# Giving the difference tiles a pool of their own, and ordering the last stage of a fused transformer kernel by hand

## The chip, the core and the metric

The kernel runs on one core of a Trainium2 chip. Its engines are TensorE (PE; weight loads are shown as PEld), VectorE (DVE), ScalarE (ACT), GpSimd (POOL) and SyncE (SP), which here only starts DMAs. The metric is the device time of one execution in microseconds, median of several runs. Times inside an execution come from a hardware profile of one of them.

## The reference

The input is `x`, 64 batches of 32 heads of 512 values, 2048 tokens in all, in float32. Two layers are applied, each with a residual:

```python
x = x + _L0_ffn_ref(_L0_cond_ref(x, lengths, ...), ...)   # long convolution, then a linear layer with routed LoRA
x = x + _L1_ffn_ref(_L1_cond_ref(x, ..., indices, 0), ...)  # gated layer with LoRA by batch, then the mixture below
```

The part that matters here is the last one, a mixture of 16 experts with two chosen for each token, beside a shared expert that all tokens use:

```python
gu_s = x2 @ shared_w_gate_up.T
g_s, u_s = jnp.split(gu_s, 2, axis=-1)
shared_out = silu(g_s) * u_s @ shared_w_down.T
...                                   # softmax, top 2, weights normalised to 1
gu = einsum('th,eih->eti', x2, w_gate_up)
act = silu(g) * u
out_e = einsum('eti,ehi->eth', act, w_down)
moe_out = einsum('eth,te->th', out_e, combine)
return moe_out + shared_out
```

## The kernel before

Tokens lie along the free dimension for most of the work: `xall` holds 4 blocks of 512 features (`NC` = 4 chunks of 128 partitions), and a token block `tb` (0 to 3) is 8 heads of all 64 batches, 512 tokens.

The first layer comes first. Then the gated layer of the second runs over 8 groups `g` of 8 batches, with 11 slices `j` of its hidden width in each. Its gate and up products use Strassen's scheme with seven products in place of eight, which needs sums of weight quarters and differences of input quarters. `differ(g)` (L789) makes the differences of a group on VectorE, in a tile `t` of the pool `l1c`; `combine_shared(j)` (L801) makes four sums of the weights of the shared expert's slice `j`, for j = 1, 2 and 3, in the last group, one call behind each of the slices 1, 2 and 3. The sums of slice 3 are made in another `t` tile and stored in DRAM (`shared_d`), because their room is wanted for other things in between. The adapters' product `lo` (L835) is made once for four slices.

After the last group `begun()` (L1140) starts the shared expert on token block 0: it finishes the last group (`past.down`, `own`, `adapt`, `turn`), closes `l1c`, opens the pool `early` with two buffers of 8 KB per partition, and makes the differences for block 0 (`differing`, L1035) in the first of them, `t_0`. `adapt` stores the group's finished rows `zt` to DRAM (`zd`) through SP's queue, just ahead of 16 loads of expert weights (`wall`). A new pool that lies over a closed one waits for the last users of all the closed pool's tiles, by the addresses of the two pools.

`shared(tb)` (L1077) runs the shared expert for one block. For slice 0 it makes gate and up by plain products (`gate_up`, L779); for slices 1 to 3 by `seven` (L1047), whose four calls of `products` write four PSUM banks; VectorE adds them up (L1064 to L1066 after the second, L1069 and L1070 after the third, L1072 and L1073 after the fourth), ScalarE applies silu (L1117) and VectorE multiplies (L1118). The down projection (L1093) of a slice follows the products of the next slice. `done(step, j)` calls a hook at a named point. PSUM has eight banks: two in the pool `ps_mm`, two in `ps_td`, four in `ps_acc`; the down projection holds those four.

The order of the work: in a `manual_schedule` region, PE, VectorE and ScalarE issue their instructions in the order in which they are written. The region runs from the start up to the end of `shared(1)`. What follows is ordered by the compiler's own planner: `worked` (L1343), which takes the 42 tiles of 128 rows through the experts, and the last stage. `issue_after` queues instructions behind a given one of the same engine.

The last stage: `shared(2)` and `shared(3)`; the gathers of each token's two expert rows from `yd` by indirect DMA on GpSimd (`rows_of`, L1414; 16 pairs of tiles, 32 gathers); the weighing of a pair (`weighed`: a scaling, L1421, and a scaled add, L1422); and `routed`, which turns the weighed rows by 64 transposes (L1441), 16 for each token block, adds them to the block's result (L1442) and stores it (L1444). A one-element memset (L1412) in front of a gather makes the gather wait for VectorE's place in the order. In this version three pairs are gathered at a time and up to four weighed at a time, behind the multiply L1118 of a slice; all 64 transposes are written behind slice 1 of `shared(3)`. The planner puts the down projection of slice 0 ahead of them and mixes that of slice 1 among them.

Of the kernel before, what the change touches and what calls it, by code (L numbers as in the profile page):

```python
# [9 lines left out]
F32 = mybir.dt.float32  # L10
I32 = mybir.dt.int32
AF = mybir.ActivationFunctionType
ALU = mybir.AluOpType
# [4 lines left out]
P = 128  # L18
B, H, L = 64, 32, 512
NS = 64  # L20
TB, NTB = 512, 4
HB = TB // B
NC = L // P
NT = B * H // P
# [5 lines left out]
NS1 = 4  # L30
# [6 lines left out]
GB = 8  # L37
NG, TG = B // GB, GB * H
# [5 lines left out]
BW = L // 2  # L44
# [59 lines left out]
def kernel(ctx: ExitStack, tc: tile.TileContext, a: dict, out: bass.AP):  # L104
    nc = tc.nc
    mm, tt, ts = nc.tensor.matmul, nc.vector.tensor_tensor, nc.vector.tensor_scalar
# [10 lines left out]
    def bank(pool, name):  # L117
        return pool.tile([P, TB], F32, tag="bank", name=name)
# [13 lines left out]
    s4 = wl0.tile([P, 5, H], F32, name="s4")  # L132
# [656 lines left out]
    def differ(g):  # L789

        b11, b12, b21, b22 = (xall[:, k : k + 2, :, lo : lo + HG] for k in (0, 2) for lo in (g * GB, g * GB + HG))
        halves.append((b11, b12, b21, b22))
        t = l1.tile([P, 4, 2, P], F32, tag="t", name=f"t_{g}")
        t1, t2, t3, t4 = (t[:, i].rearrange("p c (h b) -> p c h b", b=HG) for i in range(4))
        differences.append([t[:, i] for i in range(4)])
        tt(t1, b12, b11, ALU.subtract)
        tt(t2, b22, t1, ALU.subtract)
        tt(t3, b22, b12, ALU.subtract)
        tt(t4, b21, t2, ALU.subtract)

    def combine_shared(j):  # L801


        if j == NS1 - 1:
            ssw.append(l1.tile([P, 4 * BW], F32, tag="t", name="ssw_made"))
        a11, a12, a21, a22 = (sw[j][:, i * BW : (i + 1) * BW] for i in range(4))
        s2, s3, s4 = (ssw[j - 1][:, i * BW : (i + 1) * BW] for i in range(3))
        tt(s3, a11, a21, ALU.subtract)
        tt(a21, a21, a22, ALU.add)
        tt(s2, a21, a11, ALU.subtract)  # L810
        tt(s4, a12, s2, ALU.subtract)
        if j == NS1 - 1:
            nc.sync.dma_start(shared_d, ssw[j - 1][:, 0 : 3 * BW])

# [26 lines left out]
    kept = ctx.enter_context(tc.tile_pool(name="kept", bufs=1))  # L841
    ssw = [kept.tile([P, 3 * BW], F32, name=f"ssw_{j}") for j in range(1, NS1 - 1)]
    l1s = ExitStack()
    l1 = l1s.enter_context(tc.tile_pool(name="l1c", bufs=2))

    def batches(g, c, half=None):
# [97 lines left out]
    for g in range(NG):  # L944
# [3 lines left out]
        for j in range(NF):  # L948
# [36 lines left out]
                combine(j + 2)  # L985
            if g + 1 < NG and j == 9:
                differ(g + 1)
            if g + 1 == NG and 1 <= j < NS1:
                combine_shared(j)
            if past is not None:  # L990
                if j == 0:
                    past.adapt()
# [54 lines left out]
    def seven(tb, j, banks, si, at, done):  # L1047

        b11, b12, b21, b22 = quarters(tb)
        t1, t2, t3, t4 = diffs[tb]  # L1050
        gate, up = (x.rearrange("p (k t) -> p k t", k=2) for x in (si, at))

        def products(k, *parts):
            ps = bank(banks[k % len(banks)], f"sgu_{tb}_{j}_{k}").rearrange("p (k t) -> p k t", k=2)
            for i, (w, x) in enumerate(parts):
                w = sw[j][:, w * BW :] if w < 4 else ssw[j - 1][:, (w - 4) * BW :]
                for c in range(2):
                    mm(ps[:, i, :], w[:, c * P : (c + 1) * P], x[:, c, :], start=(c == 0), stop=(c == 1))  # L1058
            return ps

        ps = products(0, (0, b11), (6, b22))
        nc.scalar.copy(gate, ps)
        ps = products(1, (1, b21), (4, t2))
        tt(up[:, 0], gate[:, 0], ps[:, 1], ALU.add)  # L1064
        tt(gate[:, 0], gate[:, 0], ps[:, 0], ALU.add)
        tt(gate[:, 1], gate[:, 1], up[:, 0], ALU.add)  # L1066
        done("gate", j)
        ps = products(2, (3, t4), (5, t3))
        tt(up[:, 1], up[:, 0], ps[:, 1], ALU.add)  # L1069
        tt(up[:, 0], up[:, 1], ps[:, 0], ALU.add)  # L1070
        ps = products(3, (2, t1))
        tt(gate[:, 1], gate[:, 1], ps[:, 0], ALU.add)  # L1072
        tt(up[:, 1], up[:, 1], ps[:, 0], ALU.add)  # L1073
# [3 lines left out]
    def shared(tb, behind=None, midway=None, hooks=None, first=None):  # L1077
# [19 lines left out]
        for j in range(NS1):  # L1097
            if j > 0:
                si = glu.tile([P, TB], F32, tag="si", name=f"ssi_{tb}_{j}")
                at = glu.tile([P, TB], F32, tag="at", name=f"sat_{tb}_{j}")  # L1100
                seven(tb, j, (ps_mm,) if hooks else (ps_mm, ps_mm, ps_td, ps_td), si, at, done)
                pair = [si, at]
            elif first is not None:
                pair = first()
            else:
                banks = ps_mm if hooks else (ps_mm, ps_td)[j % 2]
                pair = []
                for which in range(2):
                    pair.append(bank(banks, f"sgu_{tb}_{j}_{which}"))
                    gate_up(pair[-1], tb, j, which)  # L1110
                    if which == 0:
                        done("gate", j)
            done("products", j)
            if j == 0:
                si = glu.tile([P, TB], F32, tag="si", name=f"ssi_{tb}_{j}")
                at = glu.tile([P, TB], F32, tag="at", name=f"sat_{tb}_{j}")
            nc.scalar.activation(si, pair[0], AF.Silu)  # L1117
            product = tt(at, si, pair[1], ALU.mult)  # L1118
            if j == 0 and tb == 1:
                diffs[tb] = in_place_of(0)  # L1120
                run(differing(tb, diffs[tb]))
            if j == 0:
                x1 = pools[tb // 2].tile([P, NC, TB], F32, tag="acc", name=f"x1_{tb}")
                nc.sync.dma_start(x1, x1d[tb])
                acc.append(x1)
            done("up", j)
            if behind is not None:
                with tc.issue_after(product.ins):
                    behind(j)
            if before is not None:  # L1130
                down(j - 1, before)
            before = at
            if j == 1 and midway is not None:
                midway()
# [5 lines left out]
    def begun():  # L1140
# [15 lines left out]
        gate_up(pair[1], 0, 0, 1, range(3, NC), there)  # L1156
        past.turn()
        l1s.close()
        pools.append(ctx.enter_context(tc.tile_pool(name="early", bufs=2)))
        sums = routing.enter_context(tc.tile_pool(name="ssw", bufs=1))  # L1160
        ssw[-1] = sums.tile([P, 3 * BW], F32, name="ssw_last")
        nc.gpsimd.dma_start(ssw[-1], shared_d)
# [232 lines left out]
    worked(0, NTU, ahead[0], spare=last_differences())  # L1395
    experts.close()
    wide.close()
    pools.append(ctx.enter_context(tc.tile_pool(name="late_acc", bufs=2, side="right")))
    late = ctx.enter_context(tc.tile_pool(name="late", bufs=1, side="right"))
    ssw[-1] = late.tile([P, 3 * BW], F32, name="ssw_late")  # L1400
    nc.sync.dma_start(ssw[-1], shared_d)
    with tc.tile_pool(name="fin", bufs=NT) as fin:
        order = [q * NTB + tb for tb in range(NTB) for q in range(NTB)]
        pairs = []

        def rows_of(lo, hi, held=True):

            for n in order[lo:hi]:
                g = [fin.tile([P, L], F32, tag=f"g{k}", name=f"g{k}_{n}", bufs=(NT, 6)[k]) for k in range(2)]
                for k in range(2):  # L1410
                    if held:
                        nc.vector.memset(g[k][:, 0:1], 0.0)  # L1412
                    at = bass.IndirectOffsetOnAxis(ap=posi[:, k, n : n + 1], axis=0)
                    nc.gpsimd.indirect_dma_start(g[k], None, yd[:, :], at)  # L1414
                pairs.append(g)

        def weighed(lo, hi):

            for i in range(lo, hi):
                n, g = order[i], pairs[i]  # L1420
                ts(g[0], g[0], shr[:, 0, n : n + 1], None, ALU.mult)  # L1421
                stt(g[0], g[1], shr[:, 1, n : n + 1], g[0], ALU.mult, ALU.add)  # L1422

        cuts = (0, 0, 3, 6, 9, 13, NT)

        def sums(j):
            weighed(cuts[j], cuts[j + 1])
            rows_of(3 * (j + 1), min(3 * (j + 2), NT))

        rows_of(0, 3, held=False)  # L1430
        shared(2, behind=sums)

        def routed():

            for tb in range(NTB):
                for o in range(NC):
                    ps = bank((ps_mm, ps_td)[o % 2], f"moe_{tb}_{o}")
                    by_head = ps.rearrange("p (h b) -> p h b", b=B)
                    for q in range(4):
                        src = pairs[tb * 4 + q][0][:, o * P : (o + 1) * P]  # L1440
                        nc.tensor.transpose(by_head[:, :, q * 2 * GB : (q + 1) * 2 * GB], src, ident)  # L1441
                    tt(acc[tb][:, o, :], acc[tb][:, o, :], ps, ALU.add)  # L1442
                    if tb < NTB - 1:
                        nc.sync.dma_start(out[tb, :, o, :], acc[tb][:, o, :])  # L1444

        shared(3, behind=lambda j: sums(4 + j) if j < 2 else None, midway=routed)
        for o in range(NC):
            nc.sync.dma_start(out[3, :, o, :], acc[3][:, o, :])

# [94 lines left out]
```

## Time and profile before

| what | us |
|---|---|
| median of 3 runs (1025.9 to 1026.53) | 1025.91 |
| the profiled execution | 1026.44 |
| its span, first to last instruction | 1024.7 |
| PE busy | 989.9 |
| DVE busy | 649.0 |
| ACT busy | 212.1 |
| POOL busy | 170.0 |
| mean granted PE clock, as a share | 0.998 |

The span is cut into stages at about these times: first layer to 165, groups 0 to 7 to 708, `shared(0)` and `shared(1)` to 802, the experts to 937, `shared(2)` to 974, `shared(3)` with the transposes to 1020, the last adds and stores to the end. A line of a timeline gives start, duration, engine, line of the kernel, operation, what is written and read, and in brackets the idle time before it with what seems to have released it. Successive matmuls overlap, so distances between starts say more than durations. When a wait has several causes, the one named is the one that came last in the profile.

### The profile page before, as it was taken

The page shows a single profiled execution, that of the slowest core. Times are in us where ns is not written, and L with a number is a line of the kernel's source. Part 1 is how long each engine was busy: PE and PEld are TensorE (multiplying, and loading weights), DVE is VectorE, ACT ScalarE, POOL GpSimd, SP SyncE. Part 2 cuts the span into 40 slices and gives each one's busy share as a digit, 9 for nine tenths or more (in the row PEclk, how much of TensorE's full clock was granted, in tenths as well). Part 3 has the DMA queues.
Part 4 walks back from the last instruction along what each step waited for, and adds up shares of the span by engine and source line. Part 5 has one row for each costly group of instructions (what it writes and reads, how often), then busy time and mean ns, then how long its engine had stood idle before and what let it go on. Part 6 is the DMA issues. An engine that isn't in the chain of part 4 may idle for free. (4 is left out here: it accounts for less than half of the span.)

```text
span 1024.7 us, 16925 instructions
## 1 busy us (share of the span) xinstructions
PE 989.9 (97%) x6256; PEld 794.2 (78%) x6256; DVE 649.0 (63%) x1974; ACT 212.1 (21%) x439; POOL 170.0 (17%) x189
## 2 busy tenths in 40 slices
PE   3999999999999999999999999999899999999998
PEld 1777656888898889988899898897667677776665
DVE  6656567886666776666766767764775453333775
ACT  2322111121221311224112131211100222221100
POOL 2131001210301202102012031000000322221730
PEclk9999999999999999999999999999999999999999
DMA  6566308685756746746467566531930355555752
GB/s 186 189 223 232 135 20 310 234 295 173 227 182 193 259 158 215 247 157 232 154 219 256 160 212 216 166 124 52 418 141 1 117 167 167 172 166 202 201 170 96
DMA packets 64210, 190.62 MB, mean 186 GB/s; under 512 B 8512, under 2 KB 11616, under 8 KB 63488
## 3 DMA queue, kind: packets, MB, share of 16 engines
q1 hardware_dynamic: 49360, 138.30, 39.0%
q0 software_dynamic: 14176, 51.16, 16.2%
q8 instruction: 52, 0.85, 0.3%
q14 instruction: 30, 0.25, 0.1%
q10 hardware_dynamic: 592, 0.07, 0.1%
HBM read 158.35 MB, written 31.15 MB: 185 GB/s over the span
## 5 line engine op out<-in xcount | busy, mean ns | idle before, releaser
L883 PE MATMUL zp<-wn,at 128*128 128x288 f32 x704 | 185.4, 407 | 0.4 <-DVE at L982 0.4
L818 PE MATMUL gu<-t,w 128*128 128x128 f32 x1056 | 150.2, 278 | 0.9 <-DVE gus L964 0.9
L883 PEld LDWEIGHTS zp<-wn,at 128*128 128x128 f32 x704 | 127.2, 191 | 28.5 <-DVE at L982 0.6
L818 PEld LDWEIGHTS gu<-t,w 128*128 128x128 f32 x1056 | 135.4, 192 | 14.8 <-DVE gus L964 6.4
L444 POOL DMA_INDIRECT wa<-in_la,row_a x64 | 61.1, 955 | 299.9 <-issue 183.4
L980 ACT ACTIVATE si<-gus 128x256 f32<-128x256 f32 x88 | 36.7, 417 | 352.2 <-DVE gus L978 352.2
L818 PE MATMUL gum<-xall,w 128*128 128x128 f32 x704 | 93.0, 275 | 0.0
L818 PEld LDWEIGHTS gum<-xall,w 128*128 128x128 f32 x704 | 85.7, 192 | 0.0
L1320 PE MATMUL egu<-wall,zx 128*128 x336 | 80.6, 383 | 0.3 <-issue 0.3
L964 DVE TENSOR_TENSOR gus<-gu,los 128x512 f32<-128x512 f32 x88 | 60.5, 688 | 29.8 <-PE gu L818 27.3
L958 DVE TENSOR_TENSOR los<-los 128x512 f32<-128x512 f32 (+1 forms) x72 | 46.6, 647 | 48.6 <-ACT los L838 47.0
L1320 PEld LDWEIGHTS egu<-wall,zx 128*128 128x128 f32 x336 | 60.5, 190 | 19.9 <-ACT zx L1311 13.0
L982 DVE TENSOR_TENSOR at<-si,gus 128x256 f32<-128x256 f32 x88 | 37.4, 425 | 48.2 <-ACT si L980 48.2
L1301 POOL DMA_INDIRECT zr<-zd,tok x42 | 39.7, 945 | 164.0 <-PE zrp L1309 86.3
L838 ACT COPY los<-lo 128x512 f32<-128x512 f32 (+1 forms) x96 | 46.6, 561 | 59.5 <-PE lo L835 59.5
L1093 PE MATMUL op<-sat,sw 128*128 128x512 f32 x128 | 58.0, 595 | 0.6 <-DVE sat L1118 0.3
L589 PE MATMUL main<-yT,w 128*128 128x512 f32 x128 | 58.4, 599 | 0.0
L835 PEld LDWEIGHTS lo<-rs,wb 64*128 64x128 f32 x704 | 42.9, 188 | 16.9 <-issue 11.1
L835 PE MATMUL lo<-rs,wb 64*128 64x128 f32 x704 | 48.5, 280 | 6.9 <-DVE gus L978 6.2
L818 PE MATMUL gu<-xall,w 128*128 128x128 f32 x352 | 53.7, 275 | 0.0
L818 PE MATMUL gum<-t,w 128*128 128x128 f32 x352 | 53.7, 275 | 0.0
L1340 DVE COPY eys<-ey 128x512 f32<-128x512 f32 x42 | 29.0, 691 | 29.7 <-PE ey L1338 29.7
(316 smaller groups left out, 1456.2 us busy)
## 6 DMA issues: line engine op xcount, KB each, us to landing
w<-sums_d SPq DMA_DIRECT2D x77, 512.0 KB, 4.7
w<-in_cw SPq DMA_DIRECT2D x77, 384.0 KB, 3.6
wall<-in_xw SPq DMA_DIRECT2D x16, 768.0 KB, 15.1
yd<-eys SPq DMA_DIRECT2D x42, 256.0 KB, 2.8
g<-kpad SPq DMA_DIRECT2D x15, 512.0 KB, 5.6
w<-in_cw SPq DMA_DIRECT2D x11, 512.0 KB, 4.8
sums_d<-w SPq DMA_DIRECT2D x9, 512.0 KB, 3.9
xall<-in_xT SPq DMA_DIRECT2D x4, 1024.0 KB, 8.6
```

The source lines that it names most:

```text
L444: nc.gpsimd.indirect_dma_start(to, None, src, at)
L589: mm(ps, w0[:, c, o * P : (o + 1) * P], yT[:, c, :], start=(c == 0), stop=(c == NC - 1),)
L818: mm(to, block(n, i)[:, c * P : (c + 1) * P], x[:, c], start=(c == 0), stop=(c == 1))
L835: mm(banks[which][:, at : at + P], wb[mine, lo : lo + P], r[mine, half, :], start=True, stop=True)
L838: nc.scalar.copy(to[:, first - j : first - j + n, 2 * which : 2 * which + 2], src)
L883: mm(self.zp[half][s][:, 0 : DW - TW], at[:, 1 - half, :], wn[:, j, s, lo : lo + DW - TW], start=(j == 0), stop=(j == NF - 1),)
L958: tt(lo[:, :, i], lo[:, :, i], lo[:, :, less], ALU.subtract)
L964: tt(flat, ps, adapters[:, j % 4].rearrange("p k t -> p (k t)"), ALU.add)
L982: tt(at, si, flat[:, TG:], ALU.mult)
L1093: mm(op[o], sw[j][:, i : i + P], at, start=(j == 0), stop=(j == NS1 - 1))
L1301: nc.gpsimd.indirect_dma_start(zr, None, zd[:, :], bass.IndirectOffsetOnAxis(ap=tok[:, t : t + 1], axis=0))
L1320: mm(ps[:, 0:256], x[:, c, :], wflat()[:, bass.ds(start + c * 256, 256)], start=(c == 0), stop=(c == NC - 1))
```

## The change

Four edits:

1. The `t` tiles (differences, and the sums of slice 3) move from `l1c` to a pool `dif` of their own, opened ahead of it. The pool `early` with two buffers becomes two pools `early_0` and `early_1` with one each. `t_0` and later `x1_1` lie in `early_0`, `x1_0` in `early_1`.
2. `combine_shared` becomes a generator that yields after each of its four sums; the three calls are chained in the order 3, 1, 2, and from slice 1 of the last group on each slice takes two sums (one if j is 4 or 8).
3. The last stage, from behind `worked` on, is a `manual_schedule` region for PE, VectorE and ScalarE.
4. Two pairs are gathered first. Then a `step` is taken at each of the points ("up", 0), ("gate", j), ("mid", j) and ("up", j) of `shared(2)` and `shared(3)`, where "mid" is a new hook in `seven` behind L1070. A step gathers one pair and weighs the pair gathered three steps earlier. At ("up", j), behind the step and in front of the down projection of the slice before, `routed` turns one token block, if its four pairs are weighed.

```diff
-        t = l1.tile([P, 4, 2, P], F32, tag="t", name=f"t_{g}")
+        t = dif.tile([P, 4, 2, P], F32, tag="t", name=f"t_{g}")
...
+            assert len(ssw) == j - 1
+            ssw.append(dif.tile([P, 4 * BW], F32, tag="t", name="ssw_made"))
...
-        tt(s3, a11, a21, ALU.subtract)
...
+        yield tt(s3, a11, a21, ALU.subtract)
+        yield tt(a21, a21, a22, ALU.add)
+        yield tt(s2, a21, a11, ALU.subtract)
+        yield tt(s4, a12, s2, ALU.subtract)
...
+    dif = l1s.enter_context(tc.tile_pool(name="dif", bufs=2))
     l1 = l1s.enter_context(tc.tile_pool(name="l1c", bufs=2))
...
-            if g + 1 == NG and 1 <= j < NS1:
-                combine_shared(j)
+            if g + 1 == NG and j > 0:
+                sums = sums if j > 1 else (x for k in (3, 1, 2) for x in combine_shared(k))
+                next(sums, None)
+                if j % 4:
+                    next(sums, None)
...
         tt(up[:, 1], up[:, 0], ps[:, 1], ALU.add)
         tt(up[:, 0], up[:, 1], ps[:, 0], ALU.add)
+        done("mid", j)
...
-                x1 = pools[tb // 2].tile([P, NC, TB], F32, tag="acc", name=f"x1_{tb}")
+                x1 = pools[(1, 0, 2, 2)[tb]].tile([P, NC, TB], F32, tag="acc", name=f"x1_{tb}")
...
-        pools.append(ctx.enter_context(tc.tile_pool(name="early", bufs=2)))
+        for i in range(2):
+            pools.append(ctx.enter_context(tc.tile_pool(name=f"early_{i}", bufs=1)))
...
     worked(0, NTU, ahead[0], spare=last_differences())
     experts.close()
     wide.close()
+    ctx.enter_context(tc.manual_schedule(engines=by_hand))
...
+        def step():
+            if len(pairs) < NT:
+                rows_of(order[len(pairs)])
+            if len(weighed) < NT and (len(pairs) == NT and step.last or len(weighed) < len(pairs) - 3):
+                n, g = order[len(weighed)], pairs[len(weighed)]
+                ts(g[0], g[0], shr[:, 0, n : n + 1], None, ALU.mult)
+                stt(g[0], g[1], shr[:, 1, n : n + 1], g[0], ALU.mult, ALU.add)
+                weighed.append(g[0])
+            step.last = len(pairs) == NT
...
         def routed():
+            tb = len(turned_in)
+            if tb == NTB or len(weighed) < 4 * (tb + 1):
+                return
+            turned_in.append(tb)
...
+        hooks = {("up", 0): step}
+        for j in range(1, NS1):
+            hooks |= {(x, j): step for x in ("gate", "mid")} | {("up", j): step_and_block}
+        for _ in range(2):
+            rows_of(order[len(pairs)], held=False)
+        for tb in range(2, NTB):
+            shared(tb, hooks=hooks)
```

More of the change, by code (lines that the diff above doesn't have):

```diff
@@ L804, in combine_shared @@
         if j == NS1 - 1:
-            ssw.append(l1.tile([P, 4 * BW], F32, tag="t", name="ssw_made"))
+            assert len(ssw) == j - 1
+            ssw.append(dif.tile([P, 4 * BW], F32, tag="t", name="ssw_made"))
         a11, a12, a21, a22 = (sw[j][:, i * BW : (i + 1) * BW] for i in range(4))
         s2, s3, s4 = (ssw[j - 1][:, i * BW : (i + 1) * BW] for i in range(3))
-        tt(s3, a11, a21, ALU.subtract)
-        tt(a21, a21, a22, ALU.add)
-        tt(s2, a21, a11, ALU.subtract)
-        tt(s4, a12, s2, ALU.subtract)
+        yield tt(s3, a11, a21, ALU.subtract)
+        yield tt(a21, a21, a22, ALU.add)
+        yield tt(s2, a21, a11, ALU.subtract)
+        yield tt(s4, a12, s2, ALU.subtract)
         if j == NS1 - 1:
@@ L1100, in shared @@
                 at = glu.tile([P, TB], F32, tag="at", name=f"sat_{tb}_{j}")
-                seven(tb, j, (ps_mm,) if hooks else (ps_mm, ps_mm, ps_td, ps_td), si, at, done)
+                seven(tb, j, (ps_mm,) if tb < 2 else (ps_mm, ps_mm, ps_td, ps_td), si, at, done)
                 pair = [si, at]
@@ L1105, in shared @@
             else:
-                banks = ps_mm if hooks else (ps_mm, ps_td)[j % 2]
+                banks = ps_mm if tb < 2 else (ps_mm, ps_td)[j % 2]
                 pair = []
@@ L1403 @@
         order = [q * NTB + tb for tb in range(NTB) for q in range(NTB)]
[L1404 to L1415, printed above, removed]
@@ L1417, in weighed, with rows_of @@
-        def weighed(lo, hi):
-            for i in range(lo, hi):
-                n, g = order[i], pairs[i]
+        pairs, weighed, turned_in = [], [], []
+        def rows_of(n, held=True):
+            g = [fin.tile([P, L], F32, tag=f"g{k}", name=f"g{k}_{n}", bufs=(NT, 6)[k]) for k in range(2)]
+            for k in range(2):
+                if held:
+                    nc.vector.memset(g[k][:, 0:1], 0.0)
+                at = bass.IndirectOffsetOnAxis(ap=posi[:, k, n : n + 1], axis=0)
+                nc.gpsimd.indirect_dma_start(g[k], None, yd[:, :], at)
+            pairs.append(g)
@@ L1421, in weighed @@
+        def step():
[3 more added lines that the diff above has]
+                n, g = order[len(weighed)], pairs[len(weighed)]
                 ts(g[0], g[0], shr[:, 0, n : n + 1], None, ALU.mult)
                 stt(g[0], g[1], shr[:, 1, n : n + 1], g[0], ALU.mult, ALU.add)
[L1424 to L1428, printed above, removed]
@@ L1430 @@
-        rows_of(0, 3, held=False)
-        shared(2, behind=sums)
-        def routed():
[L1435 to L1444, printed above, removed]
@@ L1446 @@
-        shared(3, behind=lambda j: sums(4 + j) if j < 2 else None, midway=routed)
+                weighed.append(g[0])
+            step.last = len(pairs) == NT
+        step.last = False
+        def routed():
+            tb = len(turned_in)
+            if tb == NTB or len(weighed) < 4 * (tb + 1):
+                return
+            turned_in.append(tb)
+            for o in range(NC):
+                ps = bank((ps_mm, ps_td)[o % 2], f"moe_{tb}_{o}")
+                by_head = ps.rearrange("p (h b) -> p h b", b=B)
+                for q in range(4):
+                    src = weighed[tb * 4 + q][:, o * P : (o + 1) * P]
+                    nc.tensor.transpose(by_head[:, :, q * 2 * GB : (q + 1) * 2 * GB], src, ident)
+                tt(acc[tb][:, o, :], acc[tb][:, o, :], ps, ALU.add)
+                if tb < NTB - 1:
+                    nc.sync.dma_start(out[tb, :, o, :], acc[tb][:, o, :])
@@ L1447, with step_and_block @@
+        def step_and_block():
+            step()
+            routed()
+        hooks = {("up", 0): step}
[5 more added lines that the diff above has]
+            shared(tb, hooks=hooks)
         for o in range(NC):
```

## The prediction, made before the changed kernel was run

> **What bounds the kernel now.** I read the page first, then busy time by stretches of 25 us, then each engine's timeline where a stretch was not full, and last the end of the kernel.
>
> ```profile
> PE 989.9 (97%) x6256; PEld 794.2 (78%) x6256; DVE 649.0 (63%) x1974; ACT 212.1 (21%) x439; POOL 170.0 (17%) x189
> ```
> TensorE is busy 97% of the span. Only its holes can be won, and any new hole is lost. Columns of the next view: stretch, length, busy time of PE, PEld, DVE, ACT, POOL, granted clock, DMA share, GB/s.
> ```profile
> 650.00:675.00 25.00, 24.11 (x187) 21.76 (x186) 20.51 (x53) 4.19 (x9) 0.00 (x0) 1.00 0.57 187
> 700.00:725.00 25.00, 21.16 (x124) 15.06 (x124) 11.77 (x33) 6.37 (x12) 0.59 (x1) 0.94 0.49 183
> 975.00:1000.00 25.00, 25.00 (x112) 16.55 (x111) 18.78 (x38) 1.81 (x3) 6.75 (x8) 1.00 0.55 178
> ```
> Two stretches that the change touches have holes, of 0.9 us and of 3.8 us (there the clock is 0.94). The end has none: from 942.6 us PE works to 1020.4; four adds and the last stores follow. The large hole, on PE and then on VectorE:
> ```profile
> 717.58 1.03 PE L1058 MATMUL sgu<-xall,ssw 128*128 128x256 f32 x4
> 721.77 1.72 PE L1058 MATMUL sgu<-xall,sw 128*128 128x256 f32 x4 [3.16 <-DVE mx L763]
> 723.28 1.91 PE L1058 MATMUL sgu<-t,ssw 128*128 128x256 f32 x4
> 724.99 1.29 PE L1058 MATMUL sgu<-t,sw 128*128 128x256 f32 x4
> 726.12 1.03 PE L1058 MATMUL sgu<-t,ssw 128*128 128x256 f32 x4
> ```
> ```profile
> 718.27 0.69 DVE L1038 TENSOR_TENSOR t<-xall 128x512 f32<-128x512 f32 x1 [5.12 <-DMA zd<-zt]
> 720.95 0.67 DVE L1118 TENSOR_TENSOR sat<-ssi,sgu 128x512 f32<-128x512 f32 x1
> ```
> VectorE stands 5.1 us before the differences of the first token block, until the store of zt has landed. It is told to run in written order, so the multiply L1118 stands behind them, and only L1118 frees the bank PE wants at 718.4. The differences do not use zt: the tile `t_0` lies in the pool `early`, over all of the closed pool `l1c`, and waits for its last user.
>
> **Rooms: -4.65 us.** With the difference tiles in a pool of their own (2 x 4 KB), `early_0` (8 KB) lies on exactly those, whose readers finished near 701. The zt stores then hold back only `x1_0`, issued by SP at 735.6 behind 16 weight loads and first read at 752.8: hidden. The differences can start when ScalarE's copy of xall ends, 713.64, and take 2.6 us (four at 0.6 to 0.7): 716.4. The copy L757 needs PE's turn at 716.9, L1118 ends at 717.8, the bank is free, and PE's next products follow the former at 718.44 without a hole. They end at 720.2. The next bank waits for ScalarE: exp at 718.2, table load 1.28, a silu 0.2, copy 0.57, so 720.6; a new hole of 0.4. The last products of this slice end at 723.2, not 727.85. Of these 4.65 us, 1.77 is clock: starts 1.51, 1.71 and 1.13 us apart where 0.86 is usual. [...] Ends 4.0 and 5.0.
>
> **Shared sums spread: -0.85 us.** The hole in the other stretch:
> ```profile
> 663.95 2.02 PE L835 MATMUL lo<-rs,wb 64*128 64x128 f32 x30 [0.89 <-DVE gus L978]
> ```
> VectorE was late with L978 by four sums of 0.42 in each of three slices. Now two follow a slice (one at j = 4), which takes 0.9 us out of each ahead of it. The later slices have 1.6 us idle before L964, so the sums moved there cost nothing; without that idle each would cost 0.45. The store of the made sums goes out in slice 3, far ahead of 718.7, when it is read back. Ends -0.9 and -0.5.
>
> **Start of the tail by hand: +1.0 us.** Before, four products of shared(2) run at 934.9 while VectorE copies the last expert's turned block (done 935.82); the last ey follows. If the hand-ordered region starts with its own first matmul, as the first region's end at 799 to 802 shows no mixing either, PE stands from 934.9 to 935.9. Ends 0 and 1.0.
>
> **Sums between the products: +10.7 us.** One slice of shared(2) before:
> ```profile
> 946.35 0.42 DVE L1064 TENSOR_TENSOR sat<-ssi,sgu 128x256 f32<-128x256 f32 x1 [2.70 <-PE sgu L1058]
> ...
> 947.14 0.42 DVE L1066 TENSOR_TENSOR ssi<-ssi,sat 128x256 f32<-128x256 f32 x1
> 948.00 0.42 DVE L1069 TENSOR_TENSOR sat<-sat,sgu 128x256 f32<-128x256 f32 x1 [0.45 <-PE sgu L1058]
> 948.46 0.42 DVE L1070 TENSOR_TENSOR sat<-sat,sgu 128x256 f32<-128x256 f32 x1
> 948.87 0.42 DVE L1072 TENSOR_TENSOR ssi<-ssi,sgu 128x256 f32<-128x256 f32 x1
> 949.21 0.41 DVE L1073 TENSOR_TENSOR sat<-sat,sgu 128x256 f32<-128x256 f32 x1
> 950.04 0.69 DVE L1118 TENSOR_TENSOR sat<-ssi,sat 128x512 f32<-128x512 f32 x1 [0.42 <-ACT ssi L1117]
> ...
> 952.77 0.48 DVE L1421 TENSOR_SCALAR g<-g,shr 128x512 f32<-128x512 f32 x1
> 953.29 0.75 DVE L1422 SCALAR_TENSOR_TENSOR g<-g,shr,g 128x512 f32<-128x512 f32 x1
> ```
> ```profile
> 947.80 1.03 PE L1058 MATMUL sgu<-xall,sw 128*128 128x256 f32 x4
> 948.67 3.60 PE L1093 MATMUL op<-sat,sw 128*128 128x512 f32 x8
> ```
> A slice is four products on PE (6.04 us), then the down projection of the slice before (3.43). VectorE follows the products closely and weighs the gathered rows afterwards; one weighing takes 952.77 to 953.99, 1.22 us, with two memsets 1.27. The change puts one weighing after L1066 ("gate"), one after L1070 ("mid") and one after L1118 ("up"), on an engine in written order. Call T the end of the fourth product (948.67 here). Then, from these rows: L1066 ends at T-1.1; gate step to T+0.15; L1070 to T+1.0; mid step to T+2.3; L1073 to T+3.1; silu from T+2.8 to T+3.4; L1118 to T+4.1; up step to T+5.4.
>
> PE goes on at T with the 16 transposes of a block (four groups of 0.44, banks in turn from ps_mm and ps_td), ahead of the down projection. Group 2 needs the ps_td bank that L1069 and L1070 read (free T+1.0), group 4 the one that L1072 and L1073 read (T+3.1). Each group also needs the block's fourth weighed tile. Steps run from 1 to 17, a weighing each from step 2; count which step makes the fourth, eighth, twelfth and sixteenth:
> Block 0, at "up" of slice 2 of shared(2): made in the gate step, in time. Group 2 waits to T+1.07, group 4 to T+3.15, end T+3.6 where the work is 1.75: 1.85 lost.
> Block 1 (slice 3) and block 2 (slice 1 of shared(3)): made in the mid step, T+2.3. Group 1 waits for it, group 4 ends at T+3.7 to 3.8: 2.0 each.
> Block 3 (slice 2 of shared(3)): its last tile is made in the up step just ahead of it, T+5.4; three transposes run, then PE stands. End T+6.8: 5.0.
> Sum 10.9; the 0.2 of holes that the old tail has (77.55 us of work from 942.62 to 1020.38) goes: +10.7. Behind each wait stand a down projection (3.43) and the next slice; nobody else can use PE. [...] If a down projection could pass, 3.43 us would cover blocks 0 to 2 and leave 1.6 of block 3: sum 1.6. No row shows PE passing; VectorE's 5.1 us wait shows written order kept. I take 10.9; ends 8 (the steps overlap as the paired weighings at 950.65 do, 1.06 each) and 13.
>
> **Clock after block 3: +1.75.** A hole of 5 us is longer than the 3.16 us row that cost 1.77. Holes of 2 us lie nearer to the 1.37 us hole at 215 us, after which the matmuls kept their pace: 0. Ends 0 and 5 (the three others too).
>
> **At nothing.** Gathers: 32 as before, 1.25 us apart on POOL; two pairs start at 942.3, then one pair a step. A pair is used three steps after its memset, some 9.5 us; landing takes 3.4 to 6.3. Steps 2 and 3 may wait 0 to 2 us for the first pairs, on VectorE in slice 1, where no transposes follow and the down projection of that slice is 5 us away; without that cover up to 2 us. The adds of a block (2.5 us) end at T+7.9, before the products after the down projection need their banks. SP: stores of blocks 0 to 2 leave earlier, in a queue that only has x1 loads. The end (adds, last stores, 4.3 us) is the same.
>
> **Sum.** 1026.44 (the profiled execution, span 1024.7) - 4.65 - 0.85 + 1.0 + 10.7 + 1.75 = 1034.4. The median of the runs is 0.53 lower than that execution: 1033.9.
>
> **The rivals.** Main case (0.64): 1031 to 1038, the ends above mixed.
> Cheaper waits (0.13): steps of 1.06, no clock loss, no hole at the start of the tail: 1026.44 - 5.5 + 8 - 0.53 = 1028.4, range 1026.5 to 1031. For it speaks that the two kinds of sum do overlap in pairs; against it that a step has only one.
> Faster (0.16): the transposes find their tiles and banks ready, or the down projections pass them. Then only 1.6 is lost there, and no clock: 1026.44 - 5.5 + 1.0 + 1.4 - 0.53 = 1022.8. It decides as soon as PE's waits in front of L1441's transposes sum to under about 4 us. VectorE's load speaks for it: 7.6 us of a slice of 9.5. Against it: a block's inputs are made at the moment of use.
> The rooms don't come free (0.07): another user of the old room, such as the store of the made sums, still holds `t_0`. Then the hole at 718 stays: 1038.6.
> A run can tell about 0.2% (2 us) from no change. Faster by more, below 1023.9: 0.16; within: 0.05; slower: 0.79. The range 1026.5 to 1038.2 leaves out the fast case and most of the last.
>
> **What would show it.** Right: the differences start near 713.7 and PE's hole near 718 is under 0.6 with the clock at 1.00; the hole before `lo` of slice 4 is gone; before L1441's transposes PE waits for VectorE four times, 2, 2, 2 and 5 us, and slow matmuls follow the last. Wrong: a tail without waits, op matmuls between the transposes as before, or `t_0` still waiting for a store.

## The result and the profile after

The changed kernel takes 1032.51 us (median of 6 runs, 1030.99 to 1033.39), the kernel before 1025.88 us beside it (6 runs): a ratio of 1.0068, 95% interval 1.0056 to 1.0079. It is 6.6 us slower. The profiled executions took 1032.49 us (span 1030.7) and 1026.44 us.

The page's first line again, then the same stretches of 25 us (columns as above), of the profile after:

```profile
PE 990.1 (96%) x6256; PEld 793.3 (77%) x6256; DVE 650.2 (63%) x1976; ACT 212.0 (21%) x439; POOL 169.0 (16%) x189
```
```profile
650.00:675.00 25.00, 25.00 (x192) 22.53 (x191) 18.95 (x50) 4.61 (x10) 0.00 (x0) 1.00 0.58 195
700.00:725.00 25.00, 24.21 (x133) 16.58 (x132) 15.66 (x51) 7.00 (x13) 0.59 (x1) 1.00 0.53 203
950.00:975.00 25.00, 22.12 (x95) 15.02 (x94) 20.15 (x50) 1.85 (x3) 13.07 (x14) 1.00 0.71 212
1000.00:1025.00 25.00, 20.72 (x75) 13.85 (x74) 13.20 (x27) 1.84 (x3) 0.00 (x0) 0.93 0.01 4
```
PE has the same work (990.1 us against 989.9). The hole at 650 is gone, the one at 700 has shrunk to 0.8 us and its clock is back at 1.00. New holes stand in the last stage, where there were none, and the clock dips there to 0.93.

The start of the shared expert, PE and VectorE, profile after:

```profile
716.49 1.03 PE L1064 MATMUL sgu<-xall,ssw 128*128 128x256 f32 x4
717.36 1.03 PE L1064 MATMUL sgu<-xall,sw 128*128 128x256 f32 x4
718.22 1.03 PE L1064 MATMUL sgu<-t,ssw 128*128 128x256 f32 x4
719.36 1.13 PE L1064 MATMUL sgu<-t,sw 128*128 128x256 f32 x4
```
```profile
712.59 0.69 DVE L1044 TENSOR_TENSOR t<-xall 128x512 f32<-128x512 f32 x1 [0.52 <-ACT xall L937]
715.96 0.68 DVE L1125 TENSOR_TENSOR sat<-ssi,sgu 128x512 f32<-128x512 f32 x1
```
The differences wait for ScalarE's copy, no longer for the store of `zt`; the products follow each other at 0.87 us, and one delay of 0.3 us remains, where the bank waits for ScalarE's copy of it, which ends at 719.31:

```profile
718.74 0.57 ACT L1068 COPY ssi<-sgu 128x512 f32<-128x512 f32 x1
```
And `lo` of slice 4 starts whole, where two of its 32 matmuls used to run ahead of a hole:

```profile
662.83 2.06 PE L836 MATMUL lo<-rs,wb 64*128 64x128 f32 x32
```

The last stage. (The change also chooses the banks by `tb < 2` where the kernel before asked `if hooks`, so that token blocks 2 and 3, which now have hooks, keep theirs.) A block is here the 16 transposes of one token block. Block 0, at slice 2 of `shared(2)`, has its tiles in time and waits for the second group's bank and the fourth's. First PE, then VectorE's last reads of these banks:

```profile
952.39 0.67 PE L1449 MATMUL moe<-cst,g 128*128 128x128 f32 x4
953.51 1.09 PE L1449 MATMUL moe<-cst,g 128*128 128x128 f32 x8 [0.46 <-DVE g L1420]
955.38 0.66 PE L1449 MATMUL moe<-cst,g 128*128 128x128 f32 x4 [0.78 <-DVE sat L1080]
```
```profile
953.04 0.42 DVE L1076 TENSOR_TENSOR sat<-sat,sgu 128x256 f32<-128x256 f32 x1
954.91 0.41 DVE L1080 TENSOR_TENSOR sat<-sat,sgu 128x256 f32<-128x256 f32 x1
```
The first wait ends with L1076 (953.46) and the memset right behind it, which the profile names; the second with L1080. Block 1, at slice 3 of `shared(2)`, waits for a tile as well. PE, then VectorE:

```profile
964.49 1.03 PE L1064 MATMUL sgu<-xall,sw 128*128 128x256 f32 x4
965.35 0.49 PE L1449 MATMUL moe<-cst,g 128*128 128x128 f32 x3
967.49 1.64 PE L1449 MATMUL moe<-cst,g 128*128 128x128 f32 x13 [1.65 <-DVE g L1432]
968.96 7.03 PE L1100 MATMUL op<-sat,sw 128*128 128x512 f32 x16
```
```profile
964.18 0.48 DVE L1431 TENSOR_SCALAR g<-g,shr 128x512 f32<-128x512 f32 x1
964.69 0.75 DVE L1432 SCALAR_TENSOR_TENSOR g<-g,shr,g 128x512 f32<-128x512 f32 x1
965.36 0.41 DVE L1075 TENSOR_TENSOR sat<-sat,sgu 128x256 f32<-128x256 f32 x1
966.16 0.48 DVE L1431 TENSOR_SCALAR g<-g,shr 128x512 f32<-128x512 f32 x1
966.68 0.75 DVE L1432 SCALAR_TENSOR_TENSOR g<-g,shr,g 128x512 f32<-128x512 f32 x1
```
Three transposes run at 965.35; the fourth needs the tile that VectorE weighs in the mid step, done at 967.43. PE then stands until 967.49, and the down projections (`op`) behind it stand as well. Block 3, at slice 2 of `shared(3)`, waits for the mid step and then for the up step, PE and VectorE's end of the latter:

```profile
1001.84 0.46 PE L1449 MATMUL moe<-cst,g 128*128 128x128 f32 x2
1003.94 0.33 PE L1449 MATMUL moe<-cst,g 128*128 128x128 f32 x1 [1.64 <-DVE g L1432]
1006.90 2.62 PE L1449 MATMUL moe<-cst,g 128*128 128x128 f32 x13 [2.63 <-DVE g L1432]
1009.32 4.34 PE L1100 MATMUL op<-sat,sw 128*128 128x512 f32 x8
1013.49 1.03 PE L1064 MATMUL sgu<-xall,sw 128*128 128x256 f32 x4
```
```profile
1006.10 0.75 DVE L1432 SCALAR_TENSOR_TENSOR g<-g,shr,g 128x512 f32<-128x512 f32 x1
```
From the first transpose to the down projection the four blocks take 3.48, 3.61, 3.62 and 7.48 us for 1.75 us of work each.

### The profile page after: what moved, and what is told of

Same layout as the page of the kernel before. It is cut to its first block, busy times and chain, and to the rows that moved or that the text cites. A ratio compares the mean times of both kernels' runs of the same rounds, so it can differ in the third digit from the quotient of the medians.

```text
span 1030.7 us, 16929 instructions
## 1 busy us (share of the span) xinstructions
PE 990.1 (96%) x6256; PEld 793.3 (77%) x6256; DVE 650.2 (63%) x1976; ACT 212.0 (21%) x439; POOL 169.0 (16%) x189
```

## The experiments

Each kernel was timed beside the kernel before on the same chip. The first eight ran on two chips (four on each) where the kernel before itself takes 1039.7 and 1040.8 us; the last four on a chip where it takes 1025.2. On the first two the profiles have pauses in the last stage, which the section on the hardware describes; the kernel before was not profiled there. So beside each ratio I give lengths read from the traces, which differ little from chip to chip where nothing pauses: from the logits of the last tokens (`lp`) to the `total` matmuls (17.58 us before, 12.88 in the change), from the first `lo` of the last group to `lp` (73.87, 72.53), and the last stage, from the twelve products L785 of `shared(2)` to PE's last matmul (83.07, 94.84).

| kernel | median us | before us | ratio (95%) | lo to lp | lp to total | last stage |
|---|---|---|---|---|---|---|
| rooms_only | 1034.63 | 1039.68 | 0.9955 (0.9938 to 0.9971) | 73.87 | 12.88 | 91.2 |
| sums_only | 1038.20 | 1039.68 | 0.9982 (0.9968 to 0.9996) | 72.53 | 17.58 | 90.5 |
| rooms_sums | 1033.89 | 1039.68 | 0.9938 (0.9919 to 0.9957) | 72.53 | 12.88 | 91.6 |
| tail_only | 1049.64 | 1039.68 | 1.0088 (1.0058 to 1.0119) | 73.87 | 18.69 | 101.4 |
| slice_later | 1033.53 | 1040.75 | 0.9927 (0.9902 to 0.9951) | 72.53 | 12.88 | 92.3 |
| sums_at_up | 1052.49 | 1040.75 | 1.0110 (1.0085 to 1.0135) | 72.53 | 12.88 | 110.2 |
| later_and_at_up | 1027.65 | 1040.75 | 0.9883 (0.9855 to 0.9911) | 72.54 | 12.87 | 84.5 |
| behind_down | 1034.37 | 1040.75 | 0.9937 (0.9913 to 0.9960) | 72.53 | 12.87 | 92.1 |
| changed_again | 1032.80 | 1025.24 | 1.0075 (1.0061 to 1.0089) | 72.53 | 12.87 | 95.4 |
| rooms_sums_again | 1019.83 | 1025.24 | 0.9944 (0.9930 to 0.9957) | 72.53 | 12.87 | 83.1 |
| later_again | 1019.10 | 1025.24 | 0.9944 (0.9930 to 0.9958) | 72.53 | 12.87 | 82.9 |
| half_gathers | 1019.78 | 1025.24 | 0.9948 (0.9934 to 0.9961) | 72.53 | 12.88 | 83.1 |

**The parts, each alone on the kernel before.** `rooms_only` has the edit of the pools:

```diff
-        t = l1.tile([P, 4, 2, P], F32, tag="t", name=f"t_{g}")
+        t = dif.tile([P, 4, 2, P], F32, tag="t", name=f"t_{g}")
...
-        pools.append(ctx.enter_context(tc.tile_pool(name="early", bufs=2)))
+        for i in range(2):
+            pools.append(ctx.enter_context(tc.tile_pool(name=f"early_{i}", bufs=1)))
```


> The kernel before with the first edit alone (pools dif, early_0, early_1). My theory: the differences no longer wait for the store of zt, the hole of 3.2 us and the half-clock behind it (1.8 us) go, a hole of 0.3 us comes: 4.7 us faster, 1021.2. Rival (the hole is only pushed to the next wait, on the weight transfers or on the list of places): 0 to 2 us faster, and a new hole between 720 and 802.

4.70 us go from the stretch between `lp` and `total`, and nothing comes back behind it (67.4 us from there to the first expert tile in every kernel). The rival falls.

`sums_only` has the generator alone:

```diff
-            if g + 1 == NG and 1 <= j < NS1:
-                combine_shared(j)
+            if g + 1 == NG and j > 0:
+                sums = sums if j > 1 else (x for k in (3, 1, 2) for x in combine_shared(k))
+                next(sums, None)
+                if j % 4:
+                    next(sums, None)
```


> The kernel before with the second edit alone (two sums of the shared weights behind each slice, from slice 1 on). My theory: the hole of 0.89 us before lo of slice 4 goes and nothing comes for it: 0.9 to 1.1 us faster, 1025.0. Rival (VectorE's sums are only moved, and hold up a later slice): 0, with a hole in slices 4 to 8.

1.34 us go from that stretch. A later slice has no new hole from the sums moved there.

`rooms_sums` has both, `tail_only` has the other two edits.

> The kernel before with the first two edits, its last stage ordered by the planner as before. My theory: the two gains add, 5.6 to 5.8 us, 1020.2, and the last stage works without a break from 937 on. Rival (the planner orders the last stage for the old start, or the gains overlap): 3 us or less.

> The kernel before with edits three and four alone (last stage by hand, a step between the products, a block turned in front of a down projection). My theory: PE waits for VectorE before the transposes for 1.8, 1.9, 1.9 and 4.7 us, and the half-clock after the last costs 1.75: 11.7 us slower, 1037.6. Rival (part of the loss of the full change comes from the earlier start of the tail, which meets transfers that have not landed): less than 10 us slower.

The two gains add: 6.04 us by the two lengths, whether the last stage is the planner's or not. On this chip the last stage of `rooms_sums` is 91.6 us in place of 83.1, against my expectation; the second run, below, shows that the kernel is not the reason. In `tail_only`, blocks 1 and 2 take 3.62 and 3.61 us, as in the full change, so the loss does not come from the tail's earlier start. Block 3 took 7.89: the same holes brought 6.83 us of half clock where the change had 3.41. The 18.69 us from `lp` to `total`, where the kernel before has 17.58, have the same reason: half clock for 6.83 us behind the old hole. Block 0 took 6.00, with a pause of that chip in it. The interval of the ratio, some 6 to 12 us, holds both the 11.7 that I expected and the rival's "under 10", so the total does not decide between them; the lengths of blocks 1 and 2 do.

**What the transposes wait for.** Two causes were in the prediction: tiles weighed at the moment of use, and banks that VectorE frees late because steps stand between its adds. `slice_later` takes the first away, `sums_at_up` the second, `later_and_at_up` both.

```diff
 # slice_later
-            if tb == NTB or len(weighed) < 4 * (tb + 1):
+            if tb == NTB or ready[0] < 4 * (tb + 1):
...
             step()
             routed()
+            ready[0] = len(weighed)
```


> The changed kernel, but a block is turned only if its four tiles were weighed by the slice before: block 0 at slice 3 of shared(2), blocks 1, 2 and 3 at slices 1, 2 and 3 of shared(3). No block waits for its tiles; the banks are as in the change. My theory: the waits for banks stay, 1.75 us for each of the first three blocks and 0.4 for the last, whose slice has no steps; no hole over 2 us, so no half-clock: 5.6 us of waits where the change has 11.7, 1026.3. Rival A (the tiles alone are the cause): no waits, 1020.5. Rival B (the banks alone): 7 us, little won but the last block, 1027.5.

```diff
 # sums_at_up
-            step()
+            for _ in range(3):
+                step()
             routed()
...
-            hooks |= {(x, j): step for x in ("gate", "mid")} | {("up", j): step_and_block}
+            hooks |= {("up", j): step_and_block}
```


> The changed kernel with all three steps of a slice behind the multiply (up) and none at gate and mid, in front of the block's transposes as before. The banks are read early; the tiles come later. My theory: waits for the fourth tile of 3.0, 4.3, 4.3 and 5.5 us, 17 in all, and two or three spells of half-clock: 1039 to 1044, slower than the change. Rival B (the banks alone are the cause): waits of 0.4 each, 1022.

```diff
 # later_and_at_up, with the hooks of sums_at_up and the test of slice_later
-            step()
             routed()
+            for _ in range(3):
+                step()
+            ready[0] = len(weighed)
```


> The changed kernel with both: three steps behind the multiply, written after the block's adds, and a block turned only if its tiles were weighed by the slice before. My theory: each block waits 0.4 us for its second bank and nothing else: 1.5 us over the tail without breaks, 1021.5 to 1022. Rival C (the order by hand costs by itself, whatever is waited for): over 1026. Rival D (gathers come late when three are asked for at once): VectorE waits for DMA and PE for it, 1024 or more.

In `slice_later` block 0 met a pause; blocks 1 to 3 take 3.29, 3.26 and 1.75 us (I had expected 0.4 of wait in the last and found none). PE, block 2:

```profile
1006.86 0.60 PE L1449 MATMUL moe<-cst,g 128*128 128x128 f32 x4
1007.78 1.09 PE L1449 MATMUL moe<-cst,g 128*128 128x128 f32 x8 [0.32 <-DVE sat L1076]
1009.63 0.65 PE L1449 MATMUL moe<-cst,g 128*128 128x128 f32 x4 [0.76 <-DVE sat L1080]
```
With the tiles ready, PE still waits for the second group's bank (read last by L1076) and the fourth's (L1080): 1.5 us a block. In slice 3 of `shared(3)`, which has no steps, nothing is waited for. In `sums_at_up` the banks are free early, but the fourth tiles come from the up steps: 8.6, 7.3, 7.4 and 8.5 us a block, with transposes at half pace in each (the last 13 take 2.73 to 2.83 us up to the down projection, 1.47 in block 1 of the change), and a pause in block 0. Rivals A and B both fall: either cause alone keeps PE waiting. The two sizes can't be set against each other, since this run weighs the tiles later than the change does; and the holes of its blocks 1 to 3 sum to 3.8, 3.8 and 4.6 us, less than the 4.3, 4.3 and 5.5 expected. In `later_and_at_up`, run again on the chip without pauses (`later_again`), each block takes 1.75 us:

```profile
1004.62 1.03 PE L1064 MATMUL sgu<-xall,sw 128*128 128x256 f32 x4
1005.48 1.91 PE L1449 MATMUL moe<-cst,g 128*128 128x128 f32 x16
1007.23 7.03 PE L1100 MATMUL op<-sat,sw 128*128 128x512 f32 x16
```
Neither cause is there, and neither is a wait; even the 0.4 us that I expected for each second bank is not. Rival C falls: order by hand costs nothing by itself here (a last stage of 82.9 us, 83.07 in the kernel before). So does rival D, late gathers: from 945 to 960 us of this run VectorE waits 0.42 to 1.48 us at a time, for PE and ScalarE, and for no gather. (The first run, on a chip with pauses, had blocks of 3.13, 1.75, 1.99 and 1.75 us.) Turning a block in front of a down projection costs nothing either, when its tiles are one slice old and VectorE's adds come first.

**What stands behind the waits.** `behind_down` keeps the steps and turns a block behind the down projection:

```diff
-            hooks |= {(x, j): step for x in ("gate", "mid")} | {("up", j): step_and_block}
+            hooks |= {(x, j): step for x in ("gate", "mid", "up")} | {("down", j - 1): routed}
```


> The changed kernel with the steps as they are, but a block is turned behind the down projection of the slice before, not in front of it. My theory: the down projection's 3.43 us cover the waits of blocks 0 to 2 for tiles and banks; block 3 still waits 1.6 us; the products after blocks 0 and 2 wait some 0.75 us for the bank of the first add: about 3 us, no half-clock, 1023.5. Rival (what is waited for only comes later by as much): 1028 or more.

Block 0 met a pause. Block 1 takes 1.75 us. Block 2 waits 0.66 us; the profile names no releaser, but the products start just as the first add of the block's result ends (1002.8), which frees a bank. Block 3 waits 1.36 us for its tile. That is close to the 0.75 and 1.6 expected: the 3.43 us of the down projection cover most of what the change leaves bare. With a pause in the last stage (92.1 us), the total of this run says nothing on it.

**Controls on a chip without pauses.**

> The changed kernel as it is, on the same chip as the next three, since the runs of the parts met pauses of all engines in the last stage that the first two profiles do not have (VectorE waited 14.3 us in rooms_sums, with nothing in the profile that released it, while gathers ran). My theory: stage by stage it shows the lengths of its first profile, 12.9 us from the logits to the totals, and in the last stage 94.8 us plus such pauses as the chip has; against the kernel before it is 6 us slower on a chip without pauses. Where there are pauses, the kernel before loses more to them than this one and the difference shrinks or turns. Rival (the pauses belong to some kernels only): with pauses for the kernel before, none here, and this one faster than before by what it lacks.

> rooms_sums once more, the same file. My theory: 6.0 us faster than before by its stages (4.7 and 1.3) on any chip; its last stage is 83.1 us on a chip without pauses and 91 with them. Rival (the pause in the last stage comes from the earlier start, 6 us sooner after the last expert's rows): it pauses where the kernel before does not, and less than 3 us is won.

> later_and_at_up once more, the same file. My theory: the same gain of 6.0 us from the first two edits and a last stage of 84 to 85 us, 1 to 1.5 us for the second banks: on a chip without pauses 4.5 to 5 us faster than before and 1 us slower than rooms_sums; on a chip with pauses as before, ahead of it by what it pauses less. Rival (the order by hand is itself better than the planner's): ahead of rooms_sums on any chip.

> rooms_sums with one of the two gathers of each pair left out (the weighing reads the first tile twice), so 16 gathers in place of 32 and half the bytes. If the pauses come from the gathers, by their load on the transfers that also bring the engines' code or by anything else of theirs, VectorE's pause in slice 3 of shared(2) goes and the last stage is 83 to 84 us where rooms_sums has 91. Rival (the pauses have nothing to do with gathers): the last stage pauses as in rooms_sums. On a chip without pauses both give 83 and nothing is told apart.

The change is 0.75% slower again, with blocks of 4.04, 3.61, 3.61 and 7.42 us. `rooms_sums` works the last stage without a pause (83.1 us), so the 91.6 us of its first run belong to that chip or that moment and not to the kernel, and the rival of the earlier start falls. `rooms_sums` and `later_and_at_up` both beat the kernel before by 0.56%, and the change by 1.3%; on this chip they cannot be told apart, though the last stage of `later_again` (82.9 us) came out shorter than the 84 to 85 expected. On the chips with pauses `later_and_at_up` stands better against the kernel before (0.9883) than `rooms_sums` does (0.9938), but the two ran on different chips, and whether the order or the pauses make that difference is not shown. `half_gathers` leaves out one of the two gathers of each pair. No pause came, so it tells nothing about them; it does show that on this chip the gathers are not what the last stage waits for (83.1 us with half of them).

## Why the prediction was right, step by step

The direction, the four waits and their causes were right; 1033.9 us was forecast, 1032.5 came. Three terms missed by 0.5 to 1.0 us, all in the same direction. By the terms of the sum:

- Rooms: -4.65 forecast, -4.70 measured (17.58 to 12.88). Both halves hold: of the hole of 3.16 us a delay of 0.3 is left, and the slow clock behind it is gone (granted 0.94 from 700 to 725 us before, 1.00 after; starts 0.87 us apart).
- Sums spread: -0.85 forecast, -1.34 measured. I took the size from the idle time in brackets, 0.89. That counts from a matmul's modelled end. By starts, `zp` at 660.54 to `gu` at 665.90 was 5.36 us before and is 4.02 after. It lies outside the ends I gave (0.9 and 0.5).
- Start of the tail by hand: +1.0 forecast, 0 measured. This step failed: the four products of `shared(2)` still run between the last expert's turn and its `ey`, as before. So this region ordered by hand does not wait for the end of what stands ahead of it, and the first region's end was no evidence for its start.

```profile
928.99 0.32 PE L1339 MATMUL eap<-cst,eat 128*128 128x128 f32 x1
929.14 1.88 PE L785 MATMUL sgu<-xall,sw 128*128 128x512 f32 x4
930.86 1.02 PE L1346 MATMUL ey<-wall,eax 128*128 x2
```
- Sums between the products: waits of 1.85, 2.0, 2.0 and 5.0 forecast; 1.73, 1.86, 1.87 and 4.73 measured (each block's length less 1.75, and 1.0 less for the slow transposes of block 3). That is 10.2; less the old stage's 0.2 it is 10.0, where 10.7 was forecast. A step takes 1.18 us, from L1431's start to the next instruction's, not 1.27. `slice_later` and `sums_at_up` show both causes, `later_and_at_up` that there is no third. No down projection passed a waiting transpose: in block 1 the `op` matmuls start at 968.96, behind the last of the 16.
- Clock after block 3: 1.75 forecast. The 13 transposes took 2.42 us in place of 1.42 and the down projection behind them 4.17 in place of 3.43: 1.74. That the size fits is partly luck. The hole was forecast as one of 5 us; it came as 1.64 and 2.63, since only two transposes had their tiles at the start and the third waited for the mid step. In `tail_only` the same holes brought twice as long a spell of half clock and cost 2.4 us. Blocks 1 and 2, with holes of 1.65, kept their pace here, but the row that I took for it, the hole of 1.37 us at 215 us, was a single case: in other runs that very hole was followed by half clock (in `sums_only` 0.69 was granted from 215 to 220 us). The last section says what the two cases differ in.
- At nothing: VectorE waits 1.0 us for the first gathered pair at 942.8, as allowed for, and PE does not. In `changed_again` that wait was 2.5 us and block 0 took 4.04 us in place of 3.48, so there some 0.6 us did reach PE. The end is the same.

By the traces the terms give -4.70 - 1.34 + 11.77 = +5.7 us; PE's last matmul ends 6.0 us later, the difference having arisen ahead of the last group. The forecast for these terms was +7.95.

## What to carry to other kernels

If an engine works in written order, the place of every instruction is also the place of a wait: before a block is put ahead of ready work, list when its last input is made and when each of its banks is read for the last time, and let both lie one round back. (Here a block took 1.75 us that way in `later_again`, and 3.5 to 7.5 in the change.) Side work belongs behind the adds that free a bank, not between them (1.5 us a block in `slice_later`). The pool that opened here over a closed one waited for the last user of all of it (VectorE 5.1 us, the kernel 4.7), so tiles that are wanted early deserve a room of their own that matches what they replace.

## What the runs showed of the hardware

On two of the chips VectorE and ScalarE paused in the last stage while gathers ran, and TensorE soon stood too. VectorE in the first run of `rooms_sums`:

```profile
951.27 0.18 DVE L1417 MEMSET g<- 128x1 f32 x4
965.71 0.42 DVE L1068 TENSOR_TENSOR sat<-ssi,sgu 128x256 f32<-128x256 f32 x1 [14.26 <-remote]
```
Its inputs, the products and ScalarE's copy, were done by 957.1, so 8.6 of the 14.3 us are pause; the copy itself (956.46) came 6 us late. "remote" says that the profile found no instruction that released it. GpSimd did not pause: it went on issuing gathers until 962.8. Three stretches of 2 us (columns as above):

```profile
956.00:958.00 2.00, 2.00 (x7) 0.80 (x6) 0.00 (x0) 0.58 (x1) 1.49 (x2) 1.00 0.73 195
960.00:962.00 2.00, 0.74 (x3) 0.37 (x2) 0.00 (x0) 0.00 (x0) 1.39 (x3) 1.00 0.72 215
964.00:966.00 2.00, 0.00 (x0) 0.00 (x0) 0.29 (x1) 0.00 (x0) 0.00 (x0) 0.50 0.31 109
```
VectorE starts again at 965.7, near the end of the gathers' transfers at 965.1. In `rooms_only` (a wait of 13.9 us) it is 969.2 and 968.4, in `sums_only` (13.0 us) 973.3 and 974.2. The second run of the same `rooms_sums` on another chip, at the same place and with the same gathers, has nothing of it. The cause stays open. The traces of those two chips record no landing of any transfer, so a wait for one would look like this too. That the engines wait for their code is another idea, but no run shows it, and what the trace records speaks against it: of the two queues that the profile calls "instruction" (q8 and q14), the transfers of that stage stand at 941.2 and 942.6, none in the pause of this run.

The clock does not ask for one long hole, and the length of a hole alone does not decide. Half clock followed a hole of 3.16 us before the change, one of 2.63 in block 3 and one of 2.38 in `behind_down`. Even 1.36 us was enough at times. The same hole in front of `lo`, before and in `sums_only`, with the matmuls behind it:

```profile
215.02 1.57 PE L835 MATMUL lo<-rs,wb 64*128 64x128 f32 x22 [1.37 <-DVE gus L978]
216.53 0.71 PE L818 MATMUL gu<-t,w 128*128 128x128 f32 x4
```
```profile
215.61 1.69 PE L835 MATMUL lo<-rs,wb 64*128 64x128 f32 x22 [1.36 <-DVE gus L978]
217.23 1.22 PE L818 MATMUL gu<-t,w 128*128 128x128 f32 x4
```
The granted clock from 215 to 220 us is 1.00 in the first and 0.69 in the second. Of 26 such holes of 1.36 to 1.37 us in these traces, 8 were followed by half clock.

Where the hole lies counts as well. In each trace the spells of half clock (0.50 granted) begin and end on one grid of 3.41 us (the end of the execution cuts the last): in `sums_only` they begin at 216.9, 353.5, 626.5, 728.9 and 974.7, which are 40, 80, 30 and 72 steps apart, and each lasts one step, in some runs two. For every step at full clock I took the share of it in which PE's records show it busy, from 30 us on in the fourteen traces, some 4000 steps. All 16 steps under 0.5 were followed by half clock, none above 0.585, and 8 of the 16 between. In the step of the hole at 215 us PE was busy for 0.60 before and for 0.58 in `sums_only`; each of the holes of 1.65 in blocks 1 and 2 of the change was parted by an edge of the grid, which left 0.68 or more. In block 3 the step with the hole of 1.64 had 0.52, and the next, with the one of 2.63, had 0.23; the step of the hole of 3.16 us had 0.10. So a short hole that falls into one step can do what a longer one spread over two does not. What settles the cases in the middle is not shown, nor what the clock itself counts.
